# A gated delta-rule decoder kernel: the 32x32 diagonal solves done in place, and attention one slot later

## The chip, the cores and the metric

The kernel runs on one core of a Trainium2 chip. The metric is the device time of one execution in microseconds (us), the median over the runs shown. Everything is fp32.

The core has five engines that run side by side, each taking its own instructions in order: PE (TensorE, matrix products; a separate row PEld shows its weight loads), DVE (VectorE), ACT (ScalarE), POOL (GpSimd) and SP (which only issues DMAs here). Engines wait for each other on semaphores. Matrix products land in PSUM[...]; DVE and ACT read it, POOL does not. All other tiles lie in SBUF, 128 partitions wide.

## The reference, cut to what matters

The reference is one decoder layer over x (16 sequences of 128 tokens, 256 wide): a linear attention, a cross attention and a routed feed-forward part, each with a layer norm behind it. The change touches the linear attention alone. With 16 key heads and 32 value heads of size 128 (two value heads share a key head) it computes, per sequence and value head:

```python
mixed = silu(causal_conv4(x @ w_qkv)); z = x @ w_z
q, k, v = split(mixed); q, k = l2norm(q) * 128**-0.5, l2norm(k)
beta = sigmoid(x @ w_b); g = -exp(A_log) * softplus(x @ w_a + dt_bias)
for t in range(128):                       # Sm: 128 x 128 state
    Sm = Sm * exp(g[t])
    delta = (v[t] - k[t] @ Sm) * beta[t]
    Sm = Sm + outer(k[t], delta)
    o[t] = q[t] @ Sm
og = o * silu(z)
out = (og * rsqrt(mean(og*og) + 1e-6) * norm_w) @ w_out
```

Over one sequence of 128 tokens this is a triangular system: the deltas of all tokens solve (1 + strictly lower triangle of decayed k·k products, times beta) u = beta v, and the output is the decayed q·k products times u.

## The kernel before

**Units and slots.** The linear attention is cut into 64 units (`NU`): one key head with its two value heads (r = 0, 1) for a batch group of G = 4 sequences. A software pipeline runs over slots `s`; in slot s a fresh unit `a` starts, and older units are at later stages: `v` (unit s-6, values), `m` (s-7), `p` (s-8), `o` (s-9, output). DELAY is 7, so there are 64 + 7 + 2 = 73 slots. In each slot the program text issues the stages in the order of the loop at L557 to L647.

**Stages of a unit.** `key_query` projects keys and queries (matmul `pjkq`), convolves them (ACT, then DVE) and applies silu. `products` multiplies k by k and q (matmul `pk`) and by the decay on DVE, giving `lp`: for both value heads and four sequences the coefficients k·k (index 0) and q·k (index 1). The four 32x32 blocks on the diagonal of k·k are copied to the group's tile `ldg`, and `clear` zeroes three of them in `lp`.

**Groups.** Four units share a `Group`, which inverts the 32x32 diagonal blocks (1 + L) of all of them together, on DVE transposes and a long series of small POOL instructions (`step`), spread over three slots as `piece(0)` to `piece(4)`. `end` transposes the inverse to `Tc` on DVE (L282) and then multiplies by beta over the key norm on POOL (L283).

**Values.** `value`/`value_end` project and convolve v, `values` transposes it (matmul `pv`) and writes `u` (ACT, L446). `block_diagonal` copies the unit's inverse blocks into `bd` (ACT, four copies, L455), a zeroed 128x128 block-diagonal matrix per value head and sequence.

**Fold.** `fold` multiplies the coefficients by that block-diagonal matrix (matmul `pc`, L467, 224 of 256 columns since the first block column of k·k is not needed) and copies the product to `cm` (ACT, L471). Because the inverse is now inside the coefficients, the block substitution needs no solve of its own.

**Substitution.** `substitute` takes three jobs (unit, value head, block st). On PE each is a 128x32 part of the array writing 32 PSUM partitions of one bank `pu` (L527), the three parts beside each other; on DVE each job then subtracts its 32x512 from u (L531). A slot has two such half steps: first (m,0,1), (p,1,2), (p,0,3), later (m,1,1), (m,0,2), (p,1,3).

**Attention and output.** `attend` multiplies u by the q·k part of `cm` (matmul `po`, L482), by silu(z) on DVE (L484) and squares on ACT (L485); `gate` makes silu(z) (matmul `pjz`); `rms` and `output` follow in the unit's last slot (matmuls `pms`, `pp`, L492, L509; DVE adds into `acc`, L513).

**Order of work.** Only POOL runs in the order of the program text here (`manual_schedule(engines={Pool})`, L556). For PE, DVE, ACT and SP a planner orders the instructions when the kernel is built, by the order of the text as priority and by its own estimate of when operands are ready. On the chip each engine then keeps that order. Single-buffered tiles (kq, sq, vT, zs, og2) and two banks for projections (`pj`), five for all else (`ps`), one for small sums (`sm`) bound how far it can run ahead.

Of the kernel before, what the change touches and what calls it, by code (L numbers as in the profile page):

```python
# [8 lines left out]
F32 = mybir.dt.float32  # L9
# [3 lines left out]
ALU = mybir.AluOpType  # L13
# [3 lines left out]
P = 128  # L17
B, S, H = 16, 128, 256
HK, HV = 16, 32
G = 4  # L20
# [4 lines left out]
U = 4  # L25
# [11 lines left out]
def bc(ap, shape):  # L37
    return ap.to_broadcast(shape)
# [3 lines left out]
def decoder_kernel(  # L42
# [74 lines left out]
    with ExitStack() as st:  # L117
# [6 lines left out]
        def bank(shape, name):  # L124
            return ps.tile(shape, F32, tag="ps", name=name)
# [87 lines left out]
                    in_=d3[b * HV : (b + 1) * HV, :, :])  # L213


        bds = [att.tile([P, 8, NB, BS], F32, name=f"bd{i}") for i in range(2)]
        for t in bds:
            pool.memset(t, 0.0)


        NU = NG * HK

        class Group:
# [7 lines left out]
            def begin(self):  # L231

                k = self.k

                def small(tag, **kw):
                    return sb.tile([P, BS], F32, tag=tag, name=f"{tag}{k}", **kw)

                g, h0 = k * U // HK, k * U % HK * 2
                bg = small("bg", bufs=1)
                vec.tensor_copy(bg.rearrange("p (h b) -> p h b", b=G),  # L240
                                beta[:, g * G : (g + 1) * G, h0 : h0 + 2 * U]
                                .rearrange("p b h -> p h b"))
                bp = small("bp", bufs=1)
                vec.transpose(bp, bg)
                self.T = sb.tile([P, BS, BS], F32, tag="Tp", bufs=1, name=f"Tp{k}")
                vec.transpose(self.T, self.ldg.rearrange("p q t -> p t q"))
                ss = small("ssk", bufs=1)
                vec.tensor_scalar(ss, self.T.rearrange("p a b -> p (a b)")[:, :: BS + 1], 1e-6,
                                  None, ALU.add)
                rk = small("rk", bufs=1)  # L250
                vec.reciprocal(rk, ss)
                vec.tensor_tensor(bp, bp, rk, ALU.mult)
                nbp = small("nbp", bufs=1)
                vec.tensor_scalar(nbp, bp, -1.0, None, ALU.mult)

                pool.tensor_tensor(self.T, self.T, bc(nbp[:, None, :], [P, BS, BS]), ALU.mult)
                self.bt = small("bt")
                vec.transpose(self.bt, bp)
                sst = small("sst", bufs=1)
                vec.transpose(sst, ss)  # L260
                self.sst = sst
# [16 lines left out]
            def end(self):  # L278
                T = self.T
                pool.memset(T.rearrange("p a b -> p (a b)")[:, :: BS + 1], 1.0)  # L280
                self.Tc = sb.tile([P, 8 * U, BS], F32, tag="Tc", bufs=1, name=f"Tc{self.k}")
                vec.transpose(self.Tc.rearrange("p q c -> p c q"), T.rearrange("p t c -> p c t"))  # L282
                pool.tensor_tensor(self.Tc, self.Tc, bc(self.bt[:, :, None], [P, 8 * U, BS]), ALU.mult)  # L283

        class Unit:

# [83 lines left out]
            def norms(self):  # L370

                sq = self.t([P], "sq", bufs=1)
                act.activation(sq, self.kq[:, :, 1, :], AF.Square)
                pss = sm_pool.tile([P, G, BS], F32, tag="sm", name=f"pss{self.n}")
                for i in range(NB):
                    blk = slice(i * BS, (i + 1) * BS)
                    pe.matmul(pss[blk].rearrange("p b t -> p (b t)"), lhsT=ones, rhs=sq[:, :, blk],
                              start=True, stop=True)
                sst = self.t([BS], "sqt", bufs=1)
                vec.transpose(sst, pss)  # L380
                self.ss = self.t([], "ss", bufs=DELAY + 4)
                vec.tensor_scalar(self.ss, sst[:, :, 0], 1e-6, 1e-6 * P, ALU.add, ALU.mult)

            def decay(self):
# [10 lines left out]
            def products(self, grp):  # L395


                self.lp = sb.tile([P, 2, G, 2, P], F32, tag="lp", bufs=DELAY + 1, name=f"lp{self.n}")
                for hf in range(2):
                    pk = bank([P, 2, 2, P], f"pk{hf}_{self.n}")  # L400
                    for b in range(2):
# [45 lines left out]
                    self.u_.append(v)  # L447


            def block_diagonal(self, grp):  # L450

                self.bd = bds[self.n % 2]
                for i in range(NB):
                    blk = slice(i * BS, (i + 1) * BS)
                    act.copy(self.bd[blk, :, i, :], grp.Tc[blk, 8 * self.u : 8 * self.u + 8, :])  # L455
                self.cm = [None, None]

            def fold(self, r):


                cm = self.t([2, P], f"cm{r}")
                for hf in range(2):
                    pc = bank([P, 2, 2, P], f"pc{r}{hf}_{self.n}")
                    for b in range(2):
                        q = r * G + hf * 2 + b

                        pe.matmul(pc[:, b].rearrange("p i t -> p (i t)")[:, BS:],  # L467
                                  lhsT=self.bd[:, q].rearrange("p i c -> p (i c)"),
                                  rhs=self.lp[:, r, hf * 2 + b].rearrange("p i t -> p (i t)")[:, BS:],
                                  start=True, stop=True)  # L470
                    act.copy(cm[:, hf * 2 : hf * 2 + 2].rearrange("p b i t -> p b (i t)")[:, :, BS:],  # L471
                             pc.rearrange("p b i t -> p b (i t)")[:, :, BS:])
                self.cm[r] = cm

            def attend(self, r):

                if r == 0:
                    self.og = self.t2("og")
                    self.og2 = self.t2("og2", bufs=1)
                po = self.bank(f"po{r}")  # L480
                for b in range(G):
                    pe.matmul(po[:, b, :], lhsT=self.u_[r][:, b, :], rhs=self.cm[r][:, b, 1, :],  # L482
                              start=True, stop=True)
                vec.tensor_tensor(self.og[:, r], po, self.zs[r], ALU.mult)  # L484
                act.activation(self.og2[:, r], self.og[:, r], AF.Square)  # L485
# [31 lines left out]
        def substitute(name, jobs):  # L517


            jobs = [(u, r, st) for u, r, st in jobs if u is not None]  # L520
            if not jobs:
                return
            pu = bank([P, G, P], name)
            for b in range(G):
                for u, r, st in jobs:
                    blk = slice(st * BS, (st + 1) * BS)
                    pe.matmul(pu[blk, b, :], lhsT=u.cm[r][:, b, 0, blk], rhs=u.u_[r][:, b, :],  # L527
                              start=True, stop=True)
            for u, r, st in jobs:
                blk = slice(st * BS, (st + 1) * BS)  # L530
                vec.tensor_tensor(u.u_[r][blk], u.u_[r][blk], pu[blk], ALU.subtract)  # L531

# [4 lines left out]
        def at(n):  # L539
            return units[n] if 0 <= n < NU else None  # L540
# [13 lines left out]


        with tc.manual_schedule(engines={mybir.EngineType.Pool}):  # L556
            for s in range(NU + DELAY + 2):  # L557
                a, v, m = at(s), at(s - DELAY + 1), at(s - DELAY)
                p, o = at(s - DELAY - 1), at(s - DELAY - 2)
                if a is not None and a.u == 0:  # L560
                    groups[s // U] = Group(s // U)
                ga = groups.get(s // U)
# [27 lines left out]
                        xTs[a.g] = transposed_x(a.g)  # L590
                if v is not None:
                    v.load_v()
                if m is not None:
                    m.load_z()
                if p is not None:
                    p.load_o()
                if m is not None:
                    m.fold(0)
                    m.fold(1)
                if a is not None:  # L600
                    a.decay()
                if o is not None:
# [5 lines left out]
                    at(s - 1).clear()  # L608
                if a is not None:
                    a.key_query(1)  # L610
                substitute(f"pu{s}_0", [(m, 0, 1), (p, 1, 2), (p, 0, 3)])
                if o is not None:
                    o.output(0, 1)
                piece(1)
                if v is not None:
                    v.value(0)
                if p is not None:
                    p.attend(0)
                if m is not None:
                    m.gate(0)  # L620
                piece(2)
                substitute(f"pu{s}_1", [(m, 1, 1), (m, 0, 2), (p, 1, 3)])
                if v is not None:
                    v.value_end(0)
                    v.value(1)
                if o is not None:
                    o.output(2, 3)
                piece(3)
                if p is not None:
                    p.attend(1)  # L630
                if m is not None:
                    m.gate(1)
                if a is not None:
                    a.norms()
                    a.products(ga)
# [2 lines left out]
                piece(4)  # L638
                if v is not None:
                    v.values(groups[v.n // U])  # L640
                    v.block_diagonal(groups[v.n // U])
                if done is not None:
                    ln_apply(*done)
                    done = None
# [637 lines left out]
```

## Time and profile before

| what | value |
|---|---|
| device time, median of 3 runs | 2298.81 us (2298.75 to 2299.71) |
| the profiled execution's own time | 2275.76 us |
| its span, first to last instruction | 2274.0 us |
| mean granted TensorE clock | 0.968 |
| linear attention: first fold to last fold (L467) | 140.1 to 1801.8 us |
| linear attention: last `output` matmul starts (L509) | 1826.9 us |
| busy in 300 to 1700 us (1400 us): DVE | 1179.04 us |
| the same: ACT | 829.77 us |
| the same: POOL | 781.26 us |
| HBM traffic over the span | 65 GB/s |

The span has three stretches: the linear attention up to about 1830 us, the cross attention to about 2065 us, and the feed-forward part. Only the first is touched. Within it the folds of unit n mark slot n + 7, so the distance from one row of folds to the next is the length of a slot.

One thing to know about PE rows: a `pe.matmul` on fp32 data shows as two MATMUL records and two weight loads, so the 8 fold products of a slot are 16 records, and one substitution of 3 jobs and 4 sequences is 24. A record's duration contains the pipeline's latency, and records overlap; the rate is read from one group's start to the next group's start.

### The profile page before, as it was taken

How to read it: one execution, taken by the hardware profiler on the slowest of the kernel's cores; microseconds unless marked ns; L12 is line 12 of the kernel's file. 1: busy time of each engine (PE TensorE's matmuls, PEld its weight loads, DVE VectorE, ACT ScalarE, POOL GpSimd, SP SyncE). 2: the span in 40 equal slices, each digit the busy share in tenths (PEclk: the TensorE clock that was granted, in tenths of full speed). 3: DMA queues.
4: the chain of work that ended last, by engine and by line, in shares of the span. 5: the costliest groups of instructions: out<-in, count | busy, mean ns of one | idle time of the engine just before them, and what ended most of it. 6: DMA issues, size and time to landing. Idle time of an engine off the chain costs nothing. (4 is left out here: it accounts for less than half of the span.)

```text
span 2274.0 us, 35080 instructions
## 1 busy us (share of the span) xinstructions
PE 2085.9 (92%) x12056; PEld 1312.4 (58%) x12056; DVE 1746.3 (77%) x3263; ACT 1235.0 (54%) x2692; POOL 1124.9 (49%) x1681
## 2 busy tenths in 40 slices
PE   5658999999999999999999999999999969999997
PEld 2435566656665565656665656666556634447874
DVE  6666888888888888889888888888865667765545
ACT  4554656565666656555656565656645426554431
POOL 1656373737464655646373737374654243253122
PEclk8879999999999999999999999999999969999998
DMA  5332111122212111122222112222101070013321
GB/s 167 106 97 65 59 59 56 56 61 66 56 58 64 61 56 56 61 61 61 58 65 60 57 56 61 61 61 56 43 29 43 20 255 1 1 45 100 105 82 60
DMA packets 140640, 150.39 MB, mean 66 GB/s; under 512 B 14184, under 2 KB 111472, under 8 KB 140464
## 3 DMA queue, kind: packets, MB, share of 16 engines
q1 hardware_dynamic: 135760, 139.56, 20.7%
q0 software_dynamic: 3072, 8.39, 1.2%
q8 instruction: 98, 1.61, 0.3%
q14 instruction: 78, 0.64, 0.1%
q10 hardware_dynamic: 1632, 0.19, 0.1%
HBM read 125.82 MB, written 22.28 MB: 65 GB/s over the span
## 5 line engine op out<-in xcount | busy, mean ns | idle before, releaser
L359 POOL TENSOR_TENSOR yv<-yv,y2v 128x508 f32<-128x508 f32 x128 | 161.6, 1262 | 372.1 <-DVE yv L351 211.0
L351 DVE SCALAR_TENSOR_TENSOR ykq<-pjkq,cw,ykq 128x500 f32<-128x500 f32 (+2 forms) x384 | 274.1, 739 | 92.5 <-ACT ykq L344 84.9
L531 DVE TENSOR_TENSOR u<-u,pu 32x512 f32<-32x512 f32 x384 | 263.5, 686 | 41.1 <-PE pu L527 33.3
L276 POOL TENSOR_TENSOR Tp<-Tp,tmp 128x30 f32<-128x30 f32 (+14 forms) x480 | 267.2, 557 | 37.6
L334 PE MATMUL pjv<-xT,wv 128*128 128x512 f32 x512 | 250.0, 610 | 28.7 <-issue 20.9
L334 PE MATMUL pjkq<-xT,wkq 128*128 128x512 f32 x512 | 248.1, 620 | 25.0 <-issue 19.9
L274 POOL TENSOR_TENSOR tmp<-Tp 128x30 f32<-128x30 f32 (+14 forms) x480 | 245.5, 512 | 30.5
L334 PE MATMUL pjz<-xT,wz 128*128 128x512 f32 x512 | 253.4, 598 | 4.8 <-issue 4.8
L509 PE MATMUL pp<-wo,og 128*128 128x256 f32 x1024 | 256.4, 392 | 0.7 <-DVE acc L513 0.7
L351 DVE SCALAR_TENSOR_TENSOR yv<-pjv,cw,yv 128x504 f32<-128x504 f32 (+1 forms) x256 | 188.0, 734 | 83.5 <-ACT y2v L348 83.3
L501 POOL TENSOR_TENSOR rstd<-var,m_half 128x8 f32<-128x8 f32 x64 | 105.2, 1644 | 263.2 <-DVE var L499 263.2
L513 DVE SCALAR_TENSOR_TENSOR acc<-pp,rstd,acc 128x256 f32<-128x256 f32 x512 | 218.1, 477 | 13.0 <-POOL rstd L501 7.0
L467 PE MATMUL pc<-lp,bd 128*128 128x224 f32 x1024 | 214.7, 361 | 2.0 <-ACT u L446 1.8
L509 PEld LDWEIGHTS pp<-wo,og 128*128 128x128 f32 x1024 | 183.9, 189 | 48.9 <-issue 28.3
L360 ACT ACTIVATE vT<-yv 128x512 f32<-128x512 f32 x128 | 80.7, 631 | 229.6 <-POOL yv L359 229.5
L467 PEld LDWEIGHTS pc<-lp,bd 128*128 128x128 f32 x1024 | 186.7, 192 | 15.1 <-ACT u L446 12.1
L344 ACT ACTIVATE yv<-pjv,cw 128x512 f32<-128x512 f32 x128 | 88.0, 687 | 192.3 <-PE pjv L334 192.3
L482 PEld LDWEIGHTS po<-cm,u 128*128 128x128 f32 x1024 | 132.3, 192 | 95.7 <-DVE u L531 59.9
L334 PEld LDWEIGHTS pjkq<-xT,wkq 128*128 128x128 f32 x512 | 92.2, 194 | 136.9 <-issue 131.6
L406 DVE TENSOR_TENSOR lp<-pk,e 128x512 f32<-128x512 f32 x256 | 162.1, 678 | 4.3 <-PE pk L403 0.8
L482 PE MATMUL po<-cm,u 128*128 128x128 f32 x1024 | 139.2, 279 | 25.3 <-DVE u L531 25.3
L389 DVE TENSOR_TENSOR_SCAN e<-dec,ident 128x512 f32<-128x512 f32 x128 | 159.7, 1287 | 0.6 <-DMA dec<-dec_d 0.6
(230 smaller groups left out, 3807.3 us busy)
## 6 DMA issues: line engine op xcount, KB each, us to landing
dec<-dec_d SPq DMA_DIRECT2D x64, 512.0 KB, 4.9
wkq<-in_L_attn_w_qkv_dram SPq DMA_DIRECT2D x128, 128.0 KB, 2.3
wv<-in_L_attn_w_qkv_dram SPq DMA_DIRECT2D x64, 256.0 KB, 2.7
wz<-in_L_attn_w_z_dram SPq DMA_DIRECT2D x64, 256.0 KB, 2.8
wo<-wo_d SPq DMA_DIRECT2D x64, 256.0 KB, 2.6
rx<-xg SPq DMA_DIRECT2D x44, 128.0 KB, 2.1
yg<-ry SPq DMA_DIRECT2D x44, 128.0 KB, 1.7
xg<-zero SPq DMA_DIRECT2D x10, 512.0 KB, 8.8
```

The lines of the kernel that those rows point to most:

```text
L274: pool.tensor_tensor(tv, bc(T[:, j + 1 :, j : j + 1], [P, n, j]), bc(T[:, j : j + 1, 0:j], [P, n, j]), ALU.mult)
L276: pool.tensor_tensor(T[:, j + 1 :, 0:j], T[:, j + 1 :, 0:j], tv, ALU.add)
L334: pe.matmul(pj.rearrange("p b t -> p (b t)"), lhsT=ws[kc], rhs=xTs[self.g][:, kc, :], start=(kc == 0), stop=(kc == 1))
L351: vec.scalar_tensor_tensor(out=y[:, :, d:], in0=pj[:, :, : P - d], scalar=c[:, k : k + 1], in1=y[:, :, d:], op0=ALU.mult, op1=ALU.add)
L359: pool.tensor_tensor(y[:, :, 1:], y[:, :, 1:], y2[:, :, 1:], ALU.add)
L389: vec.tensor_tensor_scan(out=e.rearrange("p b t -> p (b t)"), data0=self.dec[:, r, :], data1=ident4.rearrange("p b t -> p (b t)"), initial ...
L406: vec.tensor_tensor(self.lp[:, r, hf * 2 : hf * 2 + 2], pk, bc(self.e[r][:, hf * 2 : hf * 2 + 2, None, :], [P, 2, 2, P]), ALU.mult)
L467: pe.matmul(pc[:, b].rearrange("p i t -> p (i t)")[:, BS:], lhsT=self.bd[:, q].rearrange("p i c -> p (i c)"), rhs=self.lp[:, r, hf * 2 + b ...
L482: pe.matmul(po[:, b, :], lhsT=self.u_[r][:, b, :], rhs=self.cm[r][:, b, 1, :], start=True, stop=True)
L509: pe.matmul(pp[:, r, :], lhsT=self.og[:, r, b, :], rhs=self.wo[:, r, :], start=True, stop=True)
L513: vec.scalar_tensor_tensor(out=a, in0=pp[:, r, :], scalar=self.rstd[:, r, b : b + 1], in1=a, op0=ALU.mult, op1=ALU.add)
L531: vec.tensor_tensor(u.u_[r][blk], u.u_[r][blk], pu[blk], ALU.subtract)
```

## The change

The inverse is no longer folded into the coefficients. A block is solved where it stands: subtract what the earlier blocks contribute (`substitute`, now with `lp` in place of `cm`), then multiply the 32 rows of u by the inverse block (`solve`), as a 32x32 part of the array on the diagonal: rows 32·st to 32·st+31 in, the same PSUM partitions out, one bank `pt` for all four jobs. ACT copies each job's 32x512 back into u. The first block now needs a solve too, so each half step has three substitutions and four solves. `block_diagonal`, `fold`, `bd` and `cm` go. In `Group.end` the multiplication comes before the transpose; the transpose of beta (`bt`) goes.

Attention moves one slot later: the loads of z and of w_out, `gate` and `attend` are for the unit that is one older than before (`p`, `q`), and `o` becomes s-10; there is one slot more (74), and `lp` and `ss` get more buffers.

```diff
-        bds = [att.tile([P, 8, NB, BS], F32, name=f"bd{i}") for i in range(2)]
-        for t in bds:
-            pool.memset(t, 0.0)
...
-                self.bt = small("bt")
-                vec.transpose(self.bt, bp)
...
-                self.Tc = sb.tile([P, 8 * U, BS], F32, tag="Tc", bufs=1, name=f"Tc{self.k}")
-                vec.transpose(self.Tc.rearrange("p q c -> p c q"), T.rearrange("p t c -> p c t"))
-                pool.tensor_tensor(self.Tc, self.Tc, bc(self.bt[:, :, None], [P, 8 * U, BS]), ALU.mult)
+
+                pool.tensor_tensor(T, T, bc(self.bp[:, :, None], [P, BS, BS]), ALU.mult)
+                self.Tt = sb.tile([P, 8 * U, BS], F32, tag="Tt", name=f"Tt{self.k}")
+                vec.transpose(self.Tt.rearrange("p q t -> p t q"), T)
...
-                self.lp = sb.tile([P, 2, G, 2, P], F32, tag="lp", bufs=DELAY + 1, name=f"lp{self.n}")
+                self.lp = sb.tile([P, 2, G, 2, P], F32, tag="lp", bufs=DELAY + 3, name=f"lp{self.n}")
...
-            def block_diagonal(self, grp):
...
-            def fold(self, r):
...
-                    pe.matmul(po[:, b, :], lhsT=self.u_[r][:, b, :], rhs=self.cm[r][:, b, 1, :],
+                    pe.matmul(po[:, b, :], lhsT=self.u_[r][:, b, :], rhs=self.lp[:, r, b, 1, :],
...
-                    pe.matmul(pu[blk, b, :], lhsT=u.cm[r][:, b, 0, blk], rhs=u.u_[r][:, b, :],
+                    pe.matmul(pu[blk, b, :], lhsT=u.lp[:, r, b, 0, blk], rhs=u.u_[r][:, b, :],
...
+        def solve(name, jobs):
+
+            jobs = [j for j in jobs if j[0] is not None]
+            if not jobs:
+                return
+            pt = bank([P, G, P], name)
+            for b in range(G):
+                for u, r, st in jobs:
+                    blk = slice(st * BS, (st + 1) * BS)
+                    pe.matmul(pt[blk, b, :], lhsT=groups[u.n // U].Tt[blk, 8 * u.u + G * r + b, :],
+                              rhs=u.u_[r][blk, b, :], start=True, stop=True)
+            for u, r, st in jobs:
+                blk = slice(st * BS, (st + 1) * BS)
+                act.copy(u.u_[r][blk], pt[blk])
...
-            for s in range(NU + DELAY + 2):
+            for s in range(NU + DELAY + 3):
                 a, v, m = at(s), at(s - DELAY + 1), at(s - DELAY)
-                p, o = at(s - DELAY - 1), at(s - DELAY - 2)
+                p, q, o = at(s - DELAY - 1), at(s - DELAY - 2), at(s - DELAY - 3)
...
-                if m is not None:
-                    m.load_z()
                 if p is not None:
-                    p.load_o()
-                if m is not None:
-                    m.fold(0)
-                    m.fold(1)
+                    p.load_z()
+                if q is not None:
+                    q.load_o()
+                jobs = [(m, 0, 0), (p, 1, 1), (p, 0, 2), (q, 1, 3)]
+                substitute(f"pu{s}_0", jobs[1:])
...
-                substitute(f"pu{s}_0", [(m, 0, 1), (p, 1, 2), (p, 0, 3)])
+                solve(f"pt{s}_0", jobs)
                 if o is not None:
                     o.output(0, 1)
                 piece(1)
+                if q is not None:
+                    q.attend(0)
                 if v is not None:
                     v.value(0)
                 if p is not None:
-                    p.attend(0)
-                if m is not None:
-                    m.gate(0)
+                    p.gate(0)
                 piece(2)
-                substitute(f"pu{s}_1", [(m, 1, 1), (m, 0, 2), (p, 1, 3)])
+                jobs = [(m, 1, 0), (m, 0, 1), (p, 1, 2), (p, 0, 3)]
+                substitute(f"pu{s}_1", jobs[1:])
                 if v is not None:
                     v.value_end(0)
                     v.value(1)
                 if o is not None:
                     o.output(2, 3)
+                solve(f"pt{s}_1", jobs)
                 piece(3)
+                if q is not None:
+                    q.attend(1)
                 if p is not None:
-                    p.attend(1)
-                if m is not None:
-                    m.gate(1)
+                    p.gate(1)
...
-                    v.block_diagonal(groups[v.n // U])
```

More of the change, by code (lines that the diff above doesn't have):

```diff
@@ L242, in begin @@
                                 .rearrange("p b h -> p h b"))
-                bp = small("bp", bufs=1)
+                self.bp = bp = small("bp", bufs=1)
                 vec.transpose(bp, bg)
@@ L380, in norms @@
                 vec.transpose(sst, pss)
[L381 removed]
+                self.ss = self.t([], "ss", bufs=DELAY + 5)
                 vec.tensor_scalar(self.ss, sst[:, :, 0], 1e-6, 1e-6 * P, ALU.add, ALU.mult)
@@ L447, in values @@
                     self.u_.append(v)
-            def block_diagonal(self, grp):
[L452 to L456, printed above, removed]
-            def fold(self, r):
[L461 to L473, printed above, removed]
             def attend(self, r):
@@ L517, in substitute @@
         def substitute(name, jobs):
-            jobs = [(u, r, st) for u, r, st in jobs if u is not None]
+            jobs = [j for j in jobs if j[0] is not None]
             if not jobs:
@@ L531, in substitute @@
                 vec.tensor_tensor(u.u_[r][blk], u.u_[r][blk], pu[blk], ALU.subtract)
+        def solve(name, jobs):
+            jobs = [j for j in jobs if j[0] is not None]
+            if not jobs:
[9 more added lines that the diff above has]
+                act.copy(u.u_[r][blk], pt[blk])
         units = [Unit(n) for n in range(NU)]
```

## The prediction

> **What bounds the kernel now.** I read the page's first part, then the busy times by stretch, then PE's groups and the timeline of one slot inside the stretch that the change touches. The stretch from 300 to 1700 us is the steady part of the linear attention:
>
> ```profile
> 300.00:1700.00 1400.00, 1337.63 (x7958) 847.78 (x7959) 1179.04 (x2034) 829.77 (x1833) 781.26 (x1158) 1.00 0.20 58
> ```
>
> After the window's bounds and length the columns are PE, PEld, DVE, ACT, POOL, then the granted clock (1.00) and DMA. PE is busy for 1337.63 of 1400 us (95.5%), DVE for 84%, ACT for 59%, DMA for 20%. A slot, from one row of folds to the next, is 26.8 us here (301.7 to 1695.1 us for 52 slots), so PE has 1.2 us of idle in a slot and DVE 4.2. PE sets the length. Its groups in this window say what it spends and where it idles:
>
> ```profile
> L467 PE MATMUL pc<-lp,bd 128*128 128x224 f32 x848 | 177.9, 361 | 2.0 <-ACT u L446 1.8
> L527 PE MATMUL pu<-u,cm 128*32 128x128 f32 x2514 | 112.8, 276 | 0.7 <-ACT cm L471 0.7
> L482 PE MATMUL po<-cm,u 128*128 128x128 f32 x832 | 112.4, 278 | 20.7 <-DVE u L531 20.7
> L443 PE MATMUL pv<-ident,vT 128*128 128x128 f32 x424 | 64.8, 281 | 16.8 <-ACT vT L360 16.8
> ```
>
> The fold (`pc`) holds 177.9 us over 53 slots. The largest idle of PE, 20.7 us, stands before `po`: attention waits for the last DVE subtraction of its own half step. The chain of waits that ended last gives nothing here: it begins at 1828 us, behind this stretch, which everything after it waits for. So what a slot gains or loses is gained or lost by the kernel.
>
> **The prices, from one slot's timeline on PE** (start, length, group):
>
> ```profile
> 999.67 3.33 PE L467 MATMUL pc<-lp,bd 128*128 128x224 f32 x16
> 1002.93 0.64 PE L492 MATMUL pms<-og,inv_dv 128*32 128x256 f32 x8
> ...
> 1006.28 1.07 PE L527 MATMUL pu<-u,cm 128*32 128x128 f32 x24
> 1007.28 1.99 PE L509 MATMUL pp<-wo,og 128*128 128x256 f32 x8
> ...
> 1013.33 1.05 PE L482 MATMUL po<-cm,u 128*128 128x128 f32 x8
> 1014.22 1.02 PE L334 MATMUL pjz<-xT,wz 128*128 128x512 f32 x2
> ```
>
> Start to start, the fold costs 3.26 us. Eight full-array records of 128 columns (`po`) cost 0.89 us, 111 ns each. The substitution's 24 records of the same 128 columns cost 1.00 us: three 32-column parts run beside each other, 8 rounds of about 110 ns, and a start. Leaving the tiled shape costs a little more: `pp` records last 379 ns at the median and 483 at most, so I add 0.10 us: 1.10 us for such a group.
>
> **Removed from PE:** the fold, 3.26 us a slot. **Added to PE:** two solves a slot. A solve is 4 jobs x 4 sequences x 2 records = 32 records of 128 columns on four 32x32 parts. No row before shows this shape. From below, four parts side by side need 8 rounds: 0.87 us with no change of shape. From above, one after another: 32 x 0.111 = 3.55, with the change 3.7 us. The nearest rows are `pu` (three column parts, one bank) and, in the cross attention, 32-row parts:
>
> ```profile
> 1937.94 0.70 PE L770 MATMUL psc<-km,x1T 32*128 32x512 f32 x2
> 1937.96 0.70 PE L793 MATMUL pst<-qT,kt 32*128 32x512 f32 x2
> 1938.48 0.59 PE L770 MATMUL psc<-km,x1T 32*128 32x512 f32 x2
> 1938.49 0.59 PE L793 MATMUL pst<-qT,kt 32*128 32x512 f32 x2
> ```
>
> Four 32-row parts start within 0.02 us of each other and their second pass follows 0.54 us later, where one full pass of 512 columns takes about 0.48 us (`pjz` x2 from 1014.22 to 1015.18 us). So row parts do run beside each other, but each of these four writes a bank of its own. **Here a rule speaks against the change**: the Trainium skill, "TensorEngine Tiling (Array Packing)", section Restrictions and Gotchas, says that different row tiles write to different PSUM banks and cannot use one bank at the same time. The four solves of a half step share the bank `pt`. If the rule means that they take turns, a solve is 3.7 us and the change adds 2 x 3.7 - 3.26 = +4.1 us a slot. By the rows it is 2 x 1.10 - 3.26 = -1.06. I take the rows: the four parts lie on the diagonal, so no two write the same partitions, just as `pu`'s three parts share a bank without loss; and the skill's "PSUM — Partial Sum Buffer" (section PSUM bank collisions raise a hardware error) gives bank and 32-partition quadrant as the unit within which accesses collide. No trace here shows a diagonal in one bank, so the rule remains as a rival.
>
> Not every slot is bound by PE: the first ones are filling, and in the last 32.6 us PE is busy for only 27.06. I count 60 of 64: 60 x 1.06 = **64 us saved**.
>
> **ACT.** `cm` goes (97.2 us in the window, 1.83 a slot) and `bd` (83.4, 1.60). Eight copies of 32x512 from PSUM come in; a 128x512 copy from PSUM is 589 ns (`qT`), and 32x256 (`ldg`, 398) costs as much as 128x256 (`rxT`, 387), so partitions do not matter: 8 x 0.54 (`qT` is busy for 17.3 us in 32 copies) = 4.3 us. ACT gains 0.9 us on 15.8, in a slot of over 25: idle time hides it. Its risk is order, since `pu` of the next half step waits for these copies; a half step of about 13 us has to hold `pu` 1.1, subtractions 2.1, `pt` 1.1 and copies 2.3, 6.6 in all, so 6 us are left for queueing.
>
> **DVE.** Three subtractions of 686 ns per half step stay; the transposes of 2 us stay (`Tc` becomes `Tt`); `bt` saves 16 x 0.20 = 3 us, all beside PE. The first substitution now issues at the head of the slot, in front of the two scans (1.29 us each) instead of behind the key convolutions.
>
> **POOL.** The same multiplication, now in front of the transpose: POOL no longer waits for DVE's `Tc` (41.5 us in the window). Values queue behind that wait on POOL, but PE's whole wait for `vT` is 16.8 us, so I count 0 to -5 us and take 0. The two `bd` memsets are 1.9 us before any fold.
>
> **DMAs.** SP issues the same 64 loads of z and 64 of w_out, each one slot later; they land in 2.8 and 2.6 us and their users moved along. The first z load moves from slot 7 to slot 8. Cost nothing: DMA is busy for 20%.
>
> **Waits exchanged.** Attention at its later place needs solves of the half step before, so the 20.7 us before `po` (0.4 us a slot) can go. In its place `pt` waits for DVE's three subtractions, twice a slot, and behind `pt` on PE stand `pp`, `po` and the projections. From below the exchange is -25 us (`po`'s wait over the whole run is 25.3, and nothing new); from above it is the third rival. Between `pu` and `pt` stand some 4 to 5 us of PE work in both halves (`pms` and keys; values and `pp`), about what stood between `pu` and `po` (`pp` and values), but there are two such waits and the copies besides. I take 0.6 us of waits a slot for the 0.4: 64 x 0.2 = **13 us lost**.
>
> **The end.** One slot more. The last three slots now run as a chain with no fold in it: four solves with copies (about 1.1 + 1.2 to 2.3 us each, fewer jobs towards the end) come to some 12 us on the path; the last fold (3.1 us) leaves it. From 4 to 15, I take **9 us lost**.
>
> Sum: -64 + 13 + 9 = -42 us. On the profiled execution's 2275.76 us this gives 2234. The median is 23 us above that execution; I carry the difference over unchanged: 2298.81 - 42 = **2257 us**.
>
> **Rivals.**
> 1. *Forecast*, PE falls by about 1 us a slot and the slot follows: 2257, own range 2220 to 2288 (best: solves at 0.87 us, `po`'s wait gone: 60 x 1.52 + 25 - 9 = 107 saved, 2192, which I hold unlikely). For it: PE at 95.5% with the only large removal on PE. Chance 0.62.
> 2. *The diagonal parts take turns in their bank*: 64 x 4.1 + 9 = +271, 2570. It decides against the change from a solve of 1.6 us on (2 x 1.6 = 3.26). For it: the rule. Against it: the `psc`/`pst` and `pu` rows. Chance 0.10.
> 3. *Solve waits behind DVE*: the subtractions end up behind the two scans at the slot's head, PE stands at `pt` for those 2.57 us once a slot, with `po`'s 0.4 gone: -1.06 + 2.57 - 0.4 = +1.1 us, 60 x 1.1 + 9 = +75, 2374. It turns the sign from 1.3 us of new waits a slot on (1.06 + 0.4, less the 0.15 that the end costs per slot). For it: DVE is 84% busy and has products and scans just there. Against it: the subtractions come first in the text, and PE today waits for them only 0.8 us at a time. Chance 0.14.
> 4. *The slot does not follow PE*: the ring from projection through ACT and DVE back to the two `pj` banks keeps it at 26.8 us, only the end is paid: 2308. For it: DVE waits 75.8 us for `ykq` and 62.0 for `y2v` in the window, time that shorter PE work doesn't remove. Against it: ACT waits 157.7 us for `pjv`, so PE is late, not ACT. Chance 0.14.
>
> **Range and chances.** A difference within 0.2% (4.6 us) counts as none, about what a measurement of this kernel can tell. Rival 4 gives 0.05 to that band, 0.06 to slower, 0.03 to faster; 2 and 3 are slower. Faster 0.65, same 0.05, slower 0.30. From 2215 to 2355 the range holds nearly all of 1 and 4 and a third of 3; it leaves out rival 2 and the rest of 3, about 0.2.
>
> **What will show it.** Right: groups of 32 `pt` records with the next group starting 1.0 to 1.2 us later; a slot of 25.6 to 26.2 us; PE's wait before `po` under 5 us in the same window, and less than 35 us of idle before `pt` and `pu` together. Wrong: `pt` groups over 1.6 us (rival 2), PE's wait `pt` for DVE u above 1.3 us a slot (3), a slot of 26.8 us with PE below 93% (4), or an end, from the last `pv` to the last `acc`, that grows by more than 15 us.

## The result, and the profile after

The changed kernel takes 2399.27 us (median of 4 runs, 2396.96 to 2401.1); the kernel before, beside it on the same chip, takes 2298.78. The ratio is 1.0441 [1.0423, 1.0459]: slower by about 100 us, where 42 us less were forecast.

The two profiled executions differ by more than that (span 2397.5 against 2274.0 us, +123.5). The last `output` matmul of the linear attention starts at 1930.9 us against 1826.9, so +104. The other 19.5 us lie behind it, in stretches that the change doesn't touch (466.6 against 447.1 us). The experiments' own profiles have 462 to 468 us there, all but y2_first_before with 444. So the execution profiled before was a quick one in those stretches, and the +104 is what stands beside the timed +100.

The steady stretch of the changed kernel, 300 to 1700 us, with the columns as before:

```profile
300.00:1700.00 1400.00, 1287.43 (x9860) 785.60 (x9859) 1109.44 (x1920) 852.43 (x1724) 716.00 (x1094) 0.96 0.21 56
```

PE is no longer full: 1287.43 us of 1400 (92%), and that at a mean granted clock of 0.96, where it was 1337.63 at 1.00. Per slot PE is busy for 26.2 us and idle for 2.3, where it was 25.6 and 1.2: although it has less to do, its busy time has grown too. DVE and POOL are emptier in the window, since fewer slots pass. PE's groups of that window, by shape, say where it idles:

```profile
L511 PE MATMUL pt<-u,Tt 32*32 32x128 f32 x3136 | 146.9, 287 | 51.6 <-DVE u L500 51.3
L451 PE MATMUL po<-lp,u 128*128 128x128 f32 x792 | 129.4, 304 | 0.0
L496 PE MATMUL pu<-u,lp 128*32 128x128 f32 x2372 | 122.6, 288 | 0.0
L437 PE MATMUL pv<-ident,vT 128*128 128x128 f32 x392 | 58.2, 282 | 55.7 <-ACT vT L354 47.6 <-DVE acc L482 8.1
```

The wait before `po` is gone (20.7 to 0.0). In its place stand 51.3 us before `pt`, the new solve, and 55.7 before `pv` instead of 16.8. What the subtractions (L500) were late for shows among DVE's waits of that window (us in total, times, longest); the first of the two, 62.0 us before, comes up again in experiment 4:

```profile
DVE yv L345 <- ACT y2v L342: 130.1, 71, 4.6
DVE Tt L277 <- POOL Tp L275: 69.8, 12, 5.8
```

Twelve times, once per group of four slots, DVE stands for POOL at the transpose `Tt`, 5.8 us each. One such place, on POOL (start, length, group):

```profile
1020.84 0.16 POOL L273 MEMSET Tp<- 128x32 f32 x1
1021.08 1.91 POOL L275 TENSOR_TENSOR Tp<-Tp,bp 128x1024 f32<-128x1024 f32 x1
```

on DVE (in brackets the idle time just before):

```profile
1016.54 0.67 DVE L453 TENSOR_TENSOR og<-po,zs 128x512 f32<-128x512 f32 x1
1023.02 1.91 DVE L277 STREAM_TRANSPOSE Tt<-Tp 128x1024 f32<-128x1024 f32 x1 [5.81 <-POOL Tp L275]
1024.79 0.68 DVE L345 SCALAR_TENSOR_TENSOR yv<-pjv,cw,yv 128x504 f32<-128x504 f32 x1
1025.50 0.68 DVE L500 TENSOR_TENSOR u<-u,pu 32x512 f32<-32x512 f32 x1
```

and on PE:

```profile
1010.05 1.08 PE L511 MATMUL pt<-u,Tt 32*32 32x128 f32 x32
1011.05 1.99 PE L478 MATMUL pp<-wo,og 128*128 128x256 f32 x8
...
1022.48 0.40 PE L511 MATMUL pt<-u,Tt 32*32 32x128 f32 x2
1026.23 0.63 PE L511 MATMUL pt<-u,Tt 32*32 32x128 f32 x2 [3.35 <-DVE u L500]
1027.72 0.63 PE L511 MATMUL pt<-u,Tt 32*32 32x128 f32 x2 [0.86 <-DVE u L500]
1029.43 1.91 PE L511 MATMUL pt<-u,Tt 32*32 32x128 f32 x26
1032.28 2.19 PE L328 MATMUL pjz<-xT,wz 128*128 128x512 f32 x4
```

The slot begins at about 1005 us. Its first solve is undisturbed: 32 records, and `pp` begins 1.00 us later. DVE is free at 1017.2 and stands at the transpose until POOL's multiplication ends at 1023.0. Behind the transpose wait a step of the value convolution (`yv`) and then the subtractions, and behind the first of those PE waits, from 1022.9. These are three queues in order, each handing on the delay of the one ahead. In the kernel before, the same transpose came behind two such steps in DVE's order, and POOL was done ahead of it:

```profile
987.52 0.17 POOL L280 MEMSET Tp<- 128x32 f32 x1
988.09 0.73 DVE L351 SCALAR_TENSOR_TENSOR yv<-pjv,cw,yv 128x500 f32<-128x500 f32 x1
988.73 2.07 DVE L282 STREAM_TRANSPOSE Tc<-Tp 128x1024 f32<-128x1024 f32 x1
```

There POOL's last piece of the inverse had ended at 987.69, 1.04 us ahead of DVE, and the multiplication came afterwards, so DVE didn't stand.

In the changed kernel POOL's last piece ends at 1021.00, 3.8 us after DVE is free. There both engines count from the same event, the end of DVE's `var`, the sum from which `rstd` of the output's norm is made: POOL's `rstd`, which stands in its order ahead of the last pieces, now waits for it (before, then after):

```profile
978.57 1.63 POOL L501 TENSOR_TENSOR rstd<-var,m_half 128x8 f32<-128x8 f32 x1
1011.88 1.64 POOL L470 TENSOR_TENSOR rstd<-var,m_half 128x8 f32<-128x8 f32 x1 [1.67 <-DVE var L468]
```

From the end of `var` to the end of its last piece POOL takes 9.2 us (11.4 before, when `rstd` still had POOL work ahead of it). DVE comes to the transpose 5.4 us after `var`, where it was 12.4. Three subtractions (2.1 us) that stood between the two now run ahead of `var`, at the head of the slot; two `yv` steps (1.4 us) have gone behind the transpose; and 2.5 us in which DVE waited there for ACT and PE are gone. So DVE's stretch is shorter than POOL's every time, and the wait is 5.8 us in each of the twelve.

The distance from one first `pk` to the next gives the slots. Beginning behind the slot in which a group ends, the four phases of a group averaged 27.75, 26.6, 26.4 and 26.3 us before; after they are 24.4, 26.1, 27.9 and 35.6. The last is the slot in which a group ends. The mean is 28.52 instead of 26.78. The last `pk` comes at 1746.3 us instead of 1666.6 (+80), and from there to the last `pp` pass 24 us more.

### The profile page after: what moved, and what is told of

Its sections match the earlier page's. It is cut to its first block, busy times and chain, and to the rows that moved or that the text cites. A ratio compares the mean times of both kernels' runs of the same rounds, so it can differ in the third digit from the quotient of the medians.

```text
span 2397.5 us, 41225 instructions
## 1 busy us (share of the span) xinstructions
PE 2138.2 (89%) x15128; PEld 1296.1 (54%) x15128; DVE 1734.0 (72%) x3247; ACT 1326.1 (55%) x2692; POOL 1097.5 (46%) x1679
## 5 line engine op out<-in xcount | busy, mean ns | idle before, releaser
L515 ACT COPY u<-pt 32x512 f32<-32x512 f32 x512 | 294.5, 575 | 100.5 <-PE pt L511 92.2
L500 DVE TENSOR_TENSOR u<-u,pu 32x512 f32<-32x512 f32 x384 | 263.6, 686 | 63.8 <-PE pu L496 53.4
L328 PE MATMUL pjkq<-xT,wkq 128*128 128x512 f32 x512 | 250.7, 630 | 26.4 <-issue 20.6
L478 PE MATMUL pp<-wo,og 128*128 128x256 f32 x1024 | 272.4, 394 | 0.0
L345 DVE SCALAR_TENSOR_TENSOR ykq<-pjkq,cw,ykq 128x500 f32<-128x500 f32 (+2 forms) x384 | 263.3, 726 | 7.2 <-ACT ykq L338 6.1
L269 POOL TENSOR_TENSOR Tp<-Tp,tmp 128x30 f32<-128x30 f32 (+14 forms) x480 | 251.0, 523 | 37.6
L511 PE MATMUL pt<-u,Tt 32*32 32x128 f32 x4096 | 203.7, 287 | 67.1 <-DVE u L500 66.8
L267 POOL TENSOR_TENSOR tmp<-Tp 128x30 f32<-128x30 f32 (+14 forms) x480 | 234.9, 489 | 30.5
L511 PEld LDWEIGHTS pt<-u,Tt 32*32 32x32 f32 x4096 | 128.7, 110 | 179.7 <-DVE u L500 91.4
L400 DVE TENSOR_TENSOR lp<-pk,e 128x512 f32<-128x512 f32 x256 | 159.6, 678 | 14.6 <-PE pk L397 14.5
L451 PE MATMUL po<-lp,u 128*128 128x128 f32 x1024 | 165.7, 303 | 0.0
L496 PE MATMUL pu<-u,lp 128*32 128x128 f32 x3072 | 162.0, 289 | 2.9 <-POOL lp L411 2.2
L440 ACT ACTIVATE u<-pv,nk 128x128 f32<-128x128 f32 x512 | 145.0, 376 | 32.7 <-PE pv L437 31.2
```

What stands on the lines that cost most here:

```text
L267: pool.tensor_tensor(tv, bc(T[:, j + 1 :, j : j + 1], [P, n, j]), bc(T[:, j : j + 1, 0:j], [P, n, j]), ALU.mult)
L269: pool.tensor_tensor(T[:, j + 1 :, 0:j], T[:, j + 1 :, 0:j], tv, ALU.add)
L328: pe.matmul(pj.rearrange("p b t -> p (b t)"), lhsT=ws[kc], rhs=xTs[self.g][:, kc, :], start=(kc == 0), stop=(kc == 1))
L345: vec.scalar_tensor_tensor(out=y[:, :, d:], in0=pj[:, :, : P - d], scalar=c[:, k : k + 1], in1=y[:, :, d:], op0=ALU.mult, op1=ALU.add)
L451: pe.matmul(po[:, b, :], lhsT=self.u_[r][:, b, :], rhs=self.lp[:, r, b, 1, :], start=True, stop=True)
L478: pe.matmul(pp[:, r, :], lhsT=self.og[:, r, b, :], rhs=self.wo[:, r, :], start=True, stop=True)
```

## The experiments

Theory 1: the reversed order in `Group.end` puts a 1.91 us POOL multiplication in front of a DVE transpose that now comes early in DVE's order; DVE stands there, subtractions and PE stand behind it. Theory 2: the solves and the later attention themselves are too dear or badly placed. All changes are against the changed kernel unless said otherwise; ratios are to the kernel before on the same chip (its median ran from 2273 to 2299 us over the chips). Slots are means over whole groups of the steady stretch; another choice of groups moves the means by up to 0.16 us, and late_turn's last column by 0.5. The planner orders each of these kernels anew, so an edit that holds one instruction can move others.

| run | us, median | ratio | mean slot, us | slot in which a group ends, us |
|---|---|---|---|---|
| before | 2298.78 | 1 | 26.78 | 26.3 |
| after | 2399.27 | 1.0441 [1.0423, 1.0459] | 28.52 | 35.6 |
| late_turn | 2343.16 | 1.0207 [1.0174, 1.0241] | 27.60 | 31.6 |
| swap_in_before | 2286.59 | 0.9967 [0.9959, 0.9975] | 26.66 | |
| no_beta | 2355.42 | 1.0262 [1.0234, 1.029] | | 33.5 |
| late_bp | 2379.05 | 1.036 [1.0335, 1.0385] | | 35.85 |
| late_both | 2287.53 | 0.9962 [0.9948, 0.9976] | 26.67 | |
| late_both_y2 | 2284.44 | 0.9952 [0.9932, 0.9971] | | |
| y2_first | 2235.18 | 0.9737 [0.972, 0.9753] | 25.68 | 26.12 |
| y2_first_alone | 2370.0 | 1.0324 [1.0302, 1.0345] | 28.15 | 35.3 |
| y2_first_before | 2275.29 | 1.0017 [1.0002, 1.0032] | | |

**1. The transpose behind the output's last addition** (late_turn). Work and data are the same; DVE's order is held at this one place, by an ordering without a semaphore (the edit is shortened, with comments added).

```diff
-                vec.transpose(self.Tt.rearrange("p q t -> p t q"), T)
+            def turn(self, behind):        # called behind v.values, in the slot's second part
+                t = vec.transpose(self.Tt.rearrange("p q t -> p t q"), self.T)
+                if behind is not None:     # last addition into acc of output(2, 3)
+                    tc.add_manual_dep(t.ins, behind.ins.name, NoSync ...)
```

> The changed kernel, with one edit: DVE's transpose of the scaled inverse (Tt) is held behind the last add of output(2,3) in its slot, so that DVE no longer stands in front of it for POOL; all sums stay. Theory 1 (the reversed order in Group.end: multiply on POOL, then transpose on DVE, makes DVE stand 5.8 us once a group with the subtractions behind it, PE stands at pt, and the granted clock drops): the slot in which a group ends falls from 35.6 us to 26 to 28, PE's wait before pt in 300 to 1700 us falls from 51.3 to under 15 us, and the time falls by 16 x 8 = 128 us, to 2255 to 2290 us. Theory 2 (the longer chain substitution, subtraction, solve, copy is what PE waits for in every slot): the wait before pt stays above 35 us and the time within 15 us of 2399.

Measured: 1.0207, so the larger half of the loss above the kernel before is gone (1.0441 to 1.0207), but less than theory 1 expected, in all three of its figures. PE's wait before `pt` falls from 51.3 to 26.4 us, and the slot in which a group ends is still 31.6 us long. DVE's waits and PE's in that window name the next one:

```profile
DVE bp L239 <- POOL Tp L275: 57.1, 10, 5.8
...
PE pt L516 <- DVE u L505: 26.4, 28, 1.8
```

`bp` has one buffer. In the kernel before, the POOL multiplication read `bt`, a transposed copy. In the changed kernel it reads `bp` itself, and the next group's transpose into `bp` (L239) may only be written when it is done. There DVE comes to that transpose later, for the group shown above at 1035.1 us, and does not wait for it. In late_turn the planner has put it, in ten groups of the window, into the very place that `Tt` had left, between `og` and `yv`, so DVE stands for the same multiplication at another instruction. A slot in which PE never stands, the one behind such a wait, takes 24.0 us from start to start:

```profile
1005.81 0.43 PE L376 MATMUL pss<-sq,ones 128*32 128x128 f32 x8
...
1029.84 0.42 PE L376 MATMUL pss<-sq,ones 128*32 128x128 f32 x8
```

**2. The reversed order alone, in the kernel before** (swap_in_before).

```diff
-                self.bt = small("bt")
-                vec.transpose(self.bt, bp)
...
+                pool.tensor_tensor(T, T, bc(self.bp[:, :, None], [P, BS, BS]), ALU.mult)
                 vec.transpose(self.Tc.rearrange("p q c -> p c q"), T.rearrange("p t c -> p c t"))
-                pool.tensor_tensor(self.Tc, self.Tc, bc(self.bt[:, :, None], [P, 8 * U, BS]), ALU.mult)
```

> The kernel before, with only the reversed order in Group.end: beta is multiplied in on POOL first, DVE transposes after it, and bt goes. Theory 1: POOL ends its series about 1 us before DVE comes to the transpose there, so the multiplication of 1.9 us in between makes DVE stand about 1 to 3 us once a group, 16 to 48 us in all: 2310 to 2345 us. Theory 2: nothing but bt's 3 us beside PE changes, 2295 to 2303 us.

Theory 1's expectation missed: nothing is lost, and 0.33% (about 7.6 us) is even gained. The wait is there, but small:

```profile
DVE Tc L281 <- POOL Tp L280: 11.7, 13, 0.9
```

0.9 us is what the timeline of before allows: 1.91 us more on POOL against 1.04 us by which POOL was early. So the reversal by itself costs nothing where DVE comes behind POOL. It needs the changed arrivals as well, and theory 1 has to be narrowed to the two together.

**3. No multiplication on POOL** (no_beta). The inverse is not scaled by beta over the key norm, which is left out of the computation; the rest stays.

```diff
-                pool.tensor_tensor(T, T, bc(self.bp[:, :, None], [P, BS, BS]), ALU.mult)
```

> The changed kernel without POOL's multiplication by beta over the key norm in Group.end (left out, so beta is missing from the result). Theory 1: DVE stands about 1.9 us less at the transpose (5.8 to 3.9) once a group, and the subtractions behind it come as much earlier: 16 x 1.9 = 30 us and, if the clock drops less, up to 60: 2340 to 2370 us. Theory 2: 2390 to 2405 us.

Measured: 1.0262, 1.8 percentage points of the 4.4 gone, as theory 1 expected. The transpose still waits for POOL's long series:

```profile
DVE Tt L275 <- POOL Tp L273: 49.2, 13, 3.8
```

The longest wait falls from 5.8 to 3.8 us, by about the multiplication's 1.91. Of the 5.8 us, then, 1.9 are the reversal. The other 3.8 are the shorter way of DVE from `var` to the transpose (5.4 us against POOL's 9.2). The earlier place of the transpose in DVE's order is part of that and the subtractions that moved ahead of `var` are another; no run takes them apart.

**4. Both DVE transposes held back** (late_both), and **the second alone** (late_bp).

```diff
-                vec.transpose(bp, bg)
...
-                vec.transpose(self.T, self.ldg.rearrange("p q t -> p t q"))
+                first = vec.transpose(self.T, self.ldg.rearrange("p q t -> p t q"))
+                t = vec.transpose(bp, bg)
+                tc.add_manual_dep(t.ins, first.ins.name, NoSync ...)
```

> late_turn, and the next group's transpose of beta (bp, one buffer, which the multiplication in Group.end now reads until its end) held behind the transpose of its own group, so that DVE does not stand at it for POOL (57.1 us in 300 to 1700 us of late_turn, 10 times, up to 5.8 us). Theory 1 (DVE standing for POOL in the slot in which a group ends, by whichever instruction comes to POOL's result too early): that slot falls from 31.6 to 25 to 27 us, PE's wait before pt under 10 us, and the time from 2343 by 16 x 5 = 80 us, to 2250 to 2285 us, below the kernel before. Theory 2 (the longer chain in every slot): 2330 to 2345 us.

> The changed kernel with bp alone held back; the transpose Tt stays where the planner put it. Theory 1: DVE stands at Tt as before (69.8 us in 300 to 1700 us), so nothing is gained: 2390 to 2405 us. If bp's single buffer were the main cause: 2340 us or less.

late_bp alone gives 1.036, between its two expectations. DVE still stands at `Tt` (75.9 us), and the slot in which a group ends is as long as before the edit; the gain lies in the slot ahead of it (27.8 to 25.8 us), where no wait for `bp` is shown. Why that slot gets shorter wasn't traced. Both together bring 0.9962: every solve is still there and the loss is gone, so theory 2 is not its cause. The median lies 2.5 us above the expected 2250 to 2285, and the slot in which a group ends, 27.5 to 27.8 us, a little above the 25 to 27. The wait before `pt` is gone and the clock is back at 0.99, but the mean slot is still 26.67 us, and PE now stands elsewhere:

```profile
PE pv L444 <- ACT vT L361: 69.7, 39, 4.4
```

ACT's timeline in one slot shows why `vT` is late, twice:

```profile
1018.26 0.60 ACT L436 ACTIVATE zs<-pjz 128x512 f32<-128x512 f32 x1 [1.40 <-PE pjz L335]
1023.43 0.63 ACT L361 ACTIVATE vT<-yv 128x512 f32<-128x512 f32 x1 [4.58 <-POOL yv L360]
1023.97 0.67 ACT L345 ACTIVATE yv<-pjv,cw 128x512 f32<-128x512 f32 x1
1024.54 0.68 ACT L349 ACTIVATE y2v<-pjv,cw 128x508 f32<-128x508 f32 x1
1025.10 2.35 ACT L522 COPY u<-pt 32x512 f32<-32x512 f32 x4
1028.47 0.63 ACT L361 ACTIVATE vT<-yv 128x512 f32<-128x512 f32 x1 [1.01 <-POOL yv L360]
```

The silu `vT` of the first value head stands 4.58 us for POOL's addition, and behind it in ACT's order wait the two first products of the second value head (`yv`, `y2v`). Only then can DVE's convolution, POOL's addition and the second `vT` follow. On PE `pv` waits for it, with all else behind.

**5. A second buffer for y2** (late_both_y2; `bufs=1` to `bufs=2`), to see whether the buffer holds ACT back.

> late_both with two buffers for y2, the second partial sum of the value convolution, so that ACT's y2 of the second value head need not wait for POOL's add of the first. If the rest of the loss (PE's pv waits 52.7 us for ACT's vT, DVE's yv 135.8 us for ACT's y2) hangs on that buffer: 15 to 40 us below late_both. If it hangs on the order on ACT and POOL: within 5 us of late_both.

It does not: 0.9952 against 0.9962, and the wait before `pv` is 69.9 us. It is the order and not the buffer.

**6. The second value head's products in front of the first one's silu** (y2_first), on top of both and of the second buffer.

```diff
-                    y2 = self.t([P], "y2", name, bufs=1)
-                    act.activation(y2[:, :, 1:], ...)
+                    y2 = self.t([P], "y2", name, bufs=2)
+                    self.y2v = act.activation(y2[:, :, 1:], ...)
...
-                act.activation(out, y, AF.Silu)
+                t = act.activation(out, y, AF.Silu)
+                tc.add_manual_dep(t.ins, self.y2v.ins.name, NoSync ...)
...
-                    v.value_end(0)
                     v.value(1)
+                    v.value_end(0)
```

> late_both_y2 with one change of order on ACT: the second value head's y and y2 come in front of the first head's vT, which waits for POOL's add. Theory: with DVE no longer standing, what is left is PE at pv for vT (69.9 us in 300 to 1700 us), since ACT stands at the first vT for POOL and y2, DVE's sums and POOL's add of the second head are queued behind it. If so, the wait falls under 30 us, the slot from 26.7 to 25 to 26 us, and the time to 2200 to 2255 us. If pv's wait comes from POOL's own lateness or from the four copies of the solve in front of the second vT: within 10 us of 2284.

Measured: 2235.18 us, 0.9737, faster than both kernels. The steady stretch, and PE's largest wait in it:

```profile
300.00:1700.00 1400.00, 1350.23 (x10963) 829.67 (x10962) 1194.88 (x2082) 933.68 (x1892) 780.27 (x1186) 1.00 0.21 59
```

```profile
L520 PE MATMUL pt<-u,Tt 32*32 32x128 f32 x3552 | 141.1, 272 | 0.0
L505 PE MATMUL pu<-u,lp 128*32 128x128 f32 x2640 | 130.0, 278 | 0.0
L460 PE MATMUL po<-lp,u 128*128 128x128 f32 x887 | 128.4, 285 | 0.0
L446 PE MATMUL pv<-ident,vT 128*128 128x128 f32 x440 | 63.7, 278 | 41.1 <-ACT vT L361 41.1
```

PE is busy for 96.4% at a clock of 1.00. The slot is 25.68 us, 1.10 less than before. The wait before `pv` has fallen to 41.1 us, not below the 30 expected.

**7. That order without the two others** (y2_first_alone), and **that order in the kernel before** (y2_first_before, where the unused 32 columns of `cm` make room for the second y2).

> The changed kernel with two y2 buffers and that order on ACT alone; Tt and bp stay where the planner put them. If DVE standing for POOL at the end of a group is a cause of its own, it stays (about 70 us in 300 to 1700 us): 2330 to 2385 us, less gained than from late_both_y2 to y2_first or as much. If the order on ACT were the cause of both: below 2300 us.

> The kernel before with two y2 buffers and the same order on ACT as y2_first (room made by leaving the 32 columns of cm that nothing uses out of its tile). If the gain of y2_first over late_both_y2 (49 us) belongs to the order on ACT whatever the kernel: 2245 to 2270 us, and the solves themselves bring 10 to 35 us. If it only matters once PE has less to do (PE waits only 16.8 us at pv in 300 to 1700 us of the kernel before): 2280 to 2300 us, and the solves bring 45 to 65 us of y2_first's 61.

Alone it takes after from 1.0441 to 1.0324, and the slot in which a group ends stays at 35.3 us. In the kernel before it changes nothing (1.0017). So the 2.6% of y2_first are not a gain of ACT's order that was to be had anyway. The likely reading, which these two runs support but do not prove, is that the kernel with less work on PE runs into orders that the longer slot had covered.

The steps can be summed. From 1.0441, holding `Tt` takes off 2.34 points, `bp` 2.45, ACT's order with the second y2 2.25. Taken alone from after, `bp` gives 0.81 and ACT's order 1.17. What a repair is worth depends on what else still stands, and on where the planner moves the rest.

## Why the prediction was wrong

**The step that failed** is the pricing of `Group.end`: the DVE and POOL terms, which were taken as nothing. The prediction put the DVE edits down as "all beside PE", with "`Tc` becomes `Tt`", and of POOL said: "The same multiplication, now in front of the transpose: POOL no longer waits for DVE's `Tc` (41.5 us in the window)... I count 0 to -5 us and take 0." It looked at the wait that the reversal takes away and not at the one that it makes. POOL's old 41.5 us cost little: without them, and without `bt`, swap_in_before gains about 7.6 us. The new wait stands on DVE, in front of the subtractions that PE waits for: 69.8 us in the window, then, in PE, 51.3. The prediction also said that the first substitution moves in front of the scans, and gave it no price: it takes 2.1 us of DVE's work out of the stretch that DVE had in front of the transpose. And `bp`, with one buffer, got a late reader, which the prediction did not list at all; it costs nothing where DVE comes to it late, and 57.1 us of DVE's time in late_turn, where it doesn't. Holding back both transposes moves the ratio from 1.0441 to 0.9962, 4.8 points or about 110 us: the whole of the loss and a little more. A transpose called unchanged had changed its place in DVE's order. The trace of before could not show that place, but it could show the margin, 1.04 us between POOL's end and DVE's arrival, against a multiplication of 1.91 us put in between. The working owed that comparison and an upper bound for the case that DVE came earlier.

**The PE price was right.** A solve of 32 records measured 1.00 us from its start to the next group's, against 1.10 taken; so rival 2 is false. In y2_first both solves of a slot measure 1.00 (at 1008.27 and 1020.26 us). That the slot of y2_first is 1.10 us shorter, against 1.06 forecast, is in part luck: 0.82 us of it are less busy time of PE (1337.63 us over 52.3 slots before, 1350.23 over 54.5 here), the other 0.28 less idle, where the forecast had 0.2 more. y2_first also holds an order on ACT that the change does not have.

**ACT's size was right, its order not.** A copy takes 0.575 us (0.54 taken), and in y2_first PE has no wait in front of `pu` or `po`, which need the copies. "Its risk is order" named the copies; the order that hurt was `vT` in front of `y2v`, 2.2 points between late_both_y2 and y2_first.

**Waits exchanged**: taken as 0.2 us a slot more. In y2_first `po`, `pt` and `pu` have no wait left and `pv` has 41.1 us in the window, 0.75 us a slot (1400 / 25.68 = 54.5 slots). Before, `po` and `pv` together had 37.5, or 0.72 a slot (52.3 slots). So this term is near zero once the orders are mended, but in the changed kernel as it is the wait before `pt` alone is 51.3 us in 49.1 slots, 1.04 a slot.

**The end** was taken as +9, from 4 to 15, with growth over 15 from the last `pv` to the last `acc` named as the sign of being wrong. That stretch grew from 32.7 to 47.3 us, by 14.6, in after, late_both and y2_first alike: within the range, at its top, and 5.6 us over what was taken. The 24 us from the last `pk` to the last `pp` in after are more since the last full slots are in them. What in the last slots makes the 14.6 wasn't tried.

**Rival 3** has the right wait (`pt` for DVE, sign turned, 2374 us given), but not its cause: it expected the scans in every slot, and what stands in front of the subtractions is the transpose, in one slot of four. The slots without it are 24.4, 26.1 and 27.9 us long. Rival 4, a slot that does not follow PE, resembles late_both at 26.67 us: there PE stands at `pv` for the chain through ACT, DVE and POOL, and not at the two `pj` banks that the rival named.

Open: why the planner has the `Tt` transpose so early, since only the order on the chip was read and not its estimates; how much of its early arrival is its place and how much the subtractions that moved; and the 41.1 us before `pv` that remain in y2_first.

## What to carry to other kernels

When two steps on different engines are exchanged, look not only at the wait that goes but at who stands in the new one and what is queued behind it on that engine; set the margin between the two arrivals in the trace against the duration put in between. Count both arrivals from an event that both engines depend on, and ask what else the change moves into or out of that stretch. The same goes for a single-buffered tile that gets a later reader. When the engine that bounds gets less work, the orders that its length had covered come out one after another, so mend the first wait, take the profile again and read the next, and don't judge a repair by its effect alone on a kernel that still stands elsewhere. Where a planner sets the order, look in the new trace at what has come into the place of an instruction that was held back.

## What the runs showed of the hardware

PE pays twice for its wait here: in the time that it stands, and in a slower clock behind it. The windows around the wait above, with the columns as before (the clock is the third from the end):

```profile
1014.00:1022.40 8.40, 8.40 (x44) 4.44 (x41) 3.21 (x7) 4.88 (x8) 7.17 (x18) 1.00 0.19 48
1022.40:1026.20 3.80, 0.48 (x3) 0.13 (x2) 3.12 (x3) 0.01 (x1) 0.59 (x1) 0.98 0.46 138
1026.20:1030.00 3.80, 2.91 (x20) 1.81 (x24) 3.38 (x6) 1.20 (x2) 1.26 (x1) 0.50 0.00 0
1030.00:1034.00 4.00, 4.00 (x30) 2.51 (x22) 2.48 (x5) 2.54 (x5) 1.26 (x1) 0.64 0.02 4
```

After 3.35 us of idle the granted clock is 0.50 for about 4 us and still 0.64 in the next four; four `pjz` records there take 2.19 us instead of 1.88. Counted as work lost (2.91 us at half, 4.00 us at 0.64) that is 1.5 + 1.4 = some 3 us on top of the 4.2 us of standing, an estimate from these rows. Together they are about 7 of the 8.2 us by which this slot (34.4 us) is longer than the same one before (26.2). The Trainium skill, "TensorE: Matmul & The Clock Gate", in its Part 1 on the clock gate, gives about 3.4 us as the idle time behind which the clock is halved. This wait, 3.35 us long, lies close to that figure. But an unbroken idle of that length isn't needed. In late_turn PE stands for 0.84, 1.09 and 0.32 us with two records in between each time, and the clock falls as far:

```profile
996.90:1000.40 3.50, 1.25 (x11) 0.44 (x14) 3.34 (x6) 0.12 (x1) 1.26 (x1) 1.00 0.48 150
1000.40:1001.70 1.30, 1.30 (x29) 1.10 (x30) 1.28 (x4) 1.30 (x3) 0.00 (x0) 1.00 0.00 0
1001.70:1005.20 3.50, 3.50 (x11) 2.09 (x10) 3.11 (x5) 2.53 (x5) 1.18 (x1) 0.52 0.00 0
```

In late_both one unbroken wait of 2.44 us (1053.4 to 1055.8) leaves it at 1.00. No run here isolates the threshold.

The four 32x32 parts on the diagonal ran side by side in one PSUM bank: 32 records of 128 columns in 1.00 us, where one after another, at the 0.111 us of a full-array record, they would need 3.55 by estimate. So the rule weighed against this in the prediction didn't bind these four parts, which write different partitions.
